# A power operation behind the gathers of a sparse message kernel, from the eleventh row block to the end

## The chip, the cores and the metric

The kernel runs on one core of a Trainium2 chip. The metric is the device time of one launch in microseconds, as the median of several runs; for the kernel before it is 361.72 us (three runs, 361.44 to 362.11). A separate execution is recorded by the hardware profiler, and all lines of profiles in this document are from such executions. The recorded execution of the kernel before took 472.48 us, with a span of 470.8 us from its first to its last instruction, so it is a good deal longer than the runs that are timed.

## The reference, cut to what matters

There are 2708 nodes with 128 features, and a matrix `adj` of 2708 x 2708 that is almost all zeros; each row holds its mean weights. Two layers follow one another.

```python
# layer 0, hyperbolic: gamma, XW per node from x and W, then
nominator   = A_hat @ (gamma * XW)
denominator = _clamp_abs(A_hat @ (gamma - 1.0))
...                                   # norms, tanh, artanh, relu
x = _layernorm(x + layer0(x, adj, W))

# layer 1, messages
s = node_feats @ msg_w[:, :D].T
d = node_feats @ msg_w[:, D:].T
messages   = gelu(s[:, None, :] + d[None, :, :] + msg_b)
aggregated = einsum('ijd,ij->id', messages, adj)
new_feats  = concatenate([node_feats, aggregated]) @ upd_w.T + upd_b
h = gelu(new_feats) + node_feats      # layernorm, weights, and once more
x = _layernorm(x + layer1(x, adj, ...))
```

The message of a pair of nodes counts only where `adj` is not zero. The kernel therefore computes messages for the edges alone.

## The kernel before, in words

The rows of `adj` are taken in 22 blocks of 128 rows.

**Layer 0 and the search for edges (loop over b = 0 to 21).** For each block, SyncE loads the transposed block `aT` (128 x 2816 in float32, 1.4 MB; L362). TensorE multiplies it with `y` into `mp` (L369, 22 products), and ScalarE takes its sign into `sgn` (L364). `keys` turns the signs into numbers whose bits name the neighbours: a product of `sgn` with powers of two, into `kx` (L396), and VectorE's MAX8 takes the largest ones into `top` (L404). `extract` works in two steps, one and two blocks later. It makes a matrix `R` that assigns each of up to 128 edges of a tile to its row, then multiplies it with the coded bits into `sel` (L489). Out of this come, for each tile t of 128 edges, the neighbour's number `J` (L500), the row's number and the weight (`rv_of`, L497), and `F`, the edge's place in the flat matrix (L501). There are 25 lists of edges (one to four per block) with 99 tiles in all.

**Two kinds of gathers**, both through the helper `gather` (L196 to L202), both indirect DMAs that GpSimd (POOL) issues:

- The **V gathers** (L505), 99 of them: 128 single numbers of `adj` at the places `F`. They serve a check only: near the end VectorE compares `V` with the weight that came out of the extraction (L848). If anything differs, a slow dense branch at the end of the program is taken. `F` has 12 buffers, so the `F` of a list can be written when the gathers of the list 12 before it have read theirs.
- The **dd gathers** (L723), 99 of them: 128 rows of 128 features of `table`, an array in HBM that holds `d`, at the numbers `J`. They feed the messages. Tiles of edges stand in 26 groups of up to four (`work`, 24 of four, one of two, one of one), and k is the place in the group. A ring of 14 groups (`RING`) holds what has been gathered and not been used. `fetch` issues up to four gathers at a time. Tiles whose neighbours all lie in the first 1280 nodes (`soon`) need only the first part of the table and may be fetched from block 14 on (`FETCH`); all others wait until the whole table has been written.

**End of layer 0.** `layer0_end` does norms and the layernorm for 10, 10 and then 2 blocks, makes `x1`, `s3` (the `s` part in three bfloat16 limbs) and the `d` part, and writes the latter to `table` (L583).

**Messages.** `messages()` takes one group: TensorE fetches `s` to the edges by `R` (L736), VectorE builds `rv`, the weight at the edge's row (L738), and adds `s` and `dd` (L741), ScalarE applies gelu (L742), and TensorE sums up with `rv` (L751). Each call then calls `fetch` and one step of the nodes' updates (`node`, `update`, `first`, `finish`), which end in the output's DMAs.

**What sets the order.** [...] The program's framework puts the instructions of an engine in a fixed order when the kernel is built, and adds the waits between engines. `gather` with `pause=True` places one more instruction directly behind its DMA: a power operation of two constant tiles of 128 x 1 on GpSimd (`gap = half ** half`), whose result nothing reads. In the kernel before, V gathers of blocks 0 to 8 are paused (61 of 99, `PAUSED = 9`), and no dd gather is.

Of the kernel before, what the change touches and what calls it, by code (L numbers as in the profile page):

```python
# [20 lines left out]
P = 128  # L21
# [7 lines left out]
CHUNKS = [(0, 10), (10, 20), (20, 22)]  # L29
PARTS = (0, 1, 2, 2)  # L30
GROUPS = [(0, 8), (8, 6), (14, 4), (18, 2), (20, 2)]
PAUSED = 9
EARLY = 8
FETCH = 14

# [3 lines left out]
SPLIT, BITS = 10, 16  # L39
# [42 lines left out]
def hyperbolic_then_message_kernel(  # L82
# [30 lines left out]
    w0_sb, wT, rowvec, o = pk[:, :D], pk[:, D : 5 * D].rearrange("p (i d) -> p i d", d=D), {}, 5 * D  # L113
# [55 lines left out]
    J = const.tile([P, NT], U32, name="J")  # L169
    V = const.tile([P, NT], F32, name="V")  # L170
# [25 lines left out]
    def gather(o, src, at, pause=False):  # L196
        last = nc.gpsimd.indirect_dma_start(  # L197
            out=o, out_offset=None, in_=src, in_offset=bass.IndirectOffsetOnAxis(ap=at, axis=0)
        )
        if pause:  # L200
            with tc.issue_after(last.ins), tc.high_priority():
                nc.gpsimd.tensor_tensor(gap, half, half, op=OP.pow)  # L202
# [10 lines left out]
    def flat(t):  # L213
        return t.rearrange("p b d -> p (b d)")
# [98 lines left out]
    for g, n in quads:  # L313
# [5 lines left out]
        t = small.tile([P, 4, D], F32, name="work", bufs=3)  # L319
        nc.vector.tensor_mul(t[:, :n, :], mx[:, g : g + n, :], mx[:, g : g + n, :])  # L320
        nc.vector.tensor_reduce(ss_m[:, g : g + n], t[:, :n, :], axis=AX.X, op=OP.add)
    for b in range(NB):
        t = small.tile([P, D], F32, name="junk")
# [89 lines left out]
    def extract(l):  # L413

        b, groups, c0, wa, wb, t0, n, late = LISTS[l]
# [34 lines left out]
        for k, _ in parts:  # L450
            first = n - late if k and wa else 0
            dl = deg[:, l, k + 1 : k + 2]
            for k0 in range(first, n, 4):
# [3 lines left out]
                o = flat(R[:, t0 + k0 : t0 + k1, :])  # L457
# [22 lines left out]
        F = small.tile([P, TMAX], U32, name="F", bufs=12)  # L480
        step = 512 // (C + 2)
        for k0 in range(0, n, step):
            k1 = min(n, k0 + step)
            w = k1 - k0
            t = slice(t0 + k0, t0 + k1)
# [16 lines left out]
                F[:, k0:k1], J[:, t], float(b * P * N - 1), rid[:, t], op0=OP.add, op1=OP.add  # L502
            )
        for t in range(t0, t0 + n):
            gather(V[:, t : t + 1], adj.rearrange("i (j o) -> (i j) o", o=1), F[:, t - t0 : t - t0 + 1], b < PAUSED)  # L505
        known[0] = b

    x1, x1T, gd = x_sb, xT, nom
# [183 lines left out]
    early, late, soon = {}, {}, set()  # L692
# [13 lines left out]
    rooms, sums, whole = [], {}, []  # L706
# [6 lines left out]
    def fetch():  # L713

        for _ in range(4):
            ready = [v for v in (True, False) if order[v] and order[v][0][0] < done[0] + RING]
            if not whole:
                ready = [v for v in ready if v and order[v][0][2] <= known[0]]
            if not ready:
                return  # L720
            q, k, _, t = order[min(ready, key=lambda v: order[v][0])].pop(0)
            while len(rooms) <= q:
                rooms.append(edge.tile([P, 4, P], F32, name="dd", bufs=RING))  # L723
            gather(rooms[q][:, k, :], table[: SPLIT * P] if t in soon else table, J[:, t : t + 1])

    def messages():

# [15 lines left out]
        for k, (b, t, first, final, before) in enumerate(ts):  # L743
# [12 lines left out]
            elif final:  # L756
                g0, gn = group[b]
                queue.append(node(gd[:, g0 : g0 + gn, :D], b - g0, b, g0, gn, [gd[:, b, :D]] if b < EARLY else []))
        fetch()
        step()  # L760
        step(1)
# [10 lines left out]
    with tc.issue_after(setup.ins):  # L772
        for b in range(NB):
            block = layer0(b)
            next(block)
            go_on(b, 0)
            for x in placed:
                next(x, None)
            placed = []
            next(block)  # L780
            go_on(b, 1)
            for x in found:
                next(x)
            placed, found = found, []
            sgn = next(block)
            for l in of_block[b]:
                keys(l, sgn)
                found.append(extract(l))
            if b == 0 or b == NB - 1:
                for x in found:  # L790
                    next(x)
                    next(x, None)
                for x in placed:
                    next(x, None)
                found, placed = [], []
            if b >= FETCH:
                fetch()
            for b0, b1 in CHUNKS:
                if b == b1 - 1 and b1 < NB:
                    ends.append((b1, layer0_end(b0, b1)))  # L800
                    next(ends[-1][1])
# [7 lines left out]
    for _ in range(RING):  # L809
        fetch()  # L810
# [25 lines left out]
    for i, v in enumerate(seconds):  # L836
        k = v.shape[1]
# [146 lines left out]
```

## Time and profile before

| | value |
|---|---|
| time, median of 3 runs | 361.72 us |
| span of the recorded execution | 470.8 us |
| mean granted TensorE clock in it | 0.787 |
| GpSimd: V gathers (99) | 98.8 us busy |
| GpSimd: dd gathers (99) | 94.8 us busy |
| GpSimd: power operations (61) | 37.8 us busy |
| DMA queue of the gathers: packets, MB, share of 16 engines | 6336, 6.55, 5.6% |
| DMA queue of SyncE | 9502, 37.43, 21.8% |

In the profile, PE is TensorE's matmuls, PEld its weight loads, DVE VectorE, ACT ScalarE, POOL GpSimd. A row of a group has the source line, engine and operation, output and input, the number of instructions; behind the bar follow busy microseconds and the mean nanoseconds of one, and behind the next bar the idle time of the engine just before them, with what ended most of it. The page's slices divide the span into 40 equal parts, and each digit is the busy share in tenths. The chain is the sequence of work that ended last, followed back from the end.

### The profile page before, as it was taken

How to read it: one execution, taken by the hardware profiler on the slowest of the kernel's cores; microseconds unless marked ns; L12 is line 12 of the kernel's file. 1: busy time of each engine (PE TensorE's matmuls, PEld its weight loads, DVE VectorE, ACT ScalarE, POOL GpSimd, SP SyncE). 2: the span in 40 equal slices, each digit the busy share in tenths (PEclk: the TensorE clock that was granted, in tenths of full speed). 3: DMA queues.
4: the chain of work that ended last, by engine and by line, in shares of the span. 5: the costliest groups of instructions: out<-in, count | busy, mean ns of one | idle time of the engine just before them, and what ended most of it. 6: DMA issues, size and time to landing. Idle time of an engine off the chain costs nothing.

```text
span 470.8 us, 8239 instructions
## 1 busy us (share of the span) xinstructions
PE 293.5 (62%) x2603; PEld 261.0 (55%) x2603; DVE 280.4 (60%) x1580; ACT 214.0 (45%) x609; POOL 242.4 (51%) x353
## 2 busy tenths in 40 slices
PE   4249999999999931252738947655300713999840
PEld 4139988999979820142627946544200712897730
DVE  0997998868979602022224779974000411799995
ACT  2953868786959802031324773932000201334441
POOL 6200888988888877735754400226776475200000
PEclk9758999999999965568957996859555665899865
DMA  8403544646644431122413300101211121100111
GB/s 335 207 1 124 194 179 135 236 142 230 222 172 158 161 117 37 28 79 95 151 28 141 126 1 24 34 11 45 52 50 50 30 54 36 24 1 4 43 37 43
DMA packets 16029, 45.15 MB, mean 96 GB/s; under 512 B 5418, under 2 KB 10942, under 8 KB 13166
## 3 DMA queue, kind: packets, MB, share of 16 engines
q1 hardware_dynamic: 9502, 37.43, 21.8%
q0 software_dynamic: 6336, 6.55, 5.6%
q10 hardware_dynamic: 144, 0.60, 0.4%
q8 instruction: 22, 0.36, 0.3%
q14 instruction: 25, 0.20, 0.1%
HBM read 41.74 MB, written 2.83 MB: 95 GB/s over the span
## 4 chain that ended last, share of the span: by engine, by line
PE 35%; DVE 27%; another core or an unknown queue 24%; ACT 6%; issue 5%; DMA 1%; DVEq 0%; ACTq 0%
PE mp L369 17%; PE kx L396 4%; PE mp L751 3%; DVE rv L738 2%; PE X L577 2%; DVE top L404 2%; PE sel L489 2%; DVE st L600 1%; PE X L736 1%; DMA xT<-in_x_t_dram 1%; DVE dd L741 1%; DVE nom L624 1%; PE kx L317 1%; PE sel L608 1%
## 5 line engine op out<-in xcount | busy, mean ns | idle before, releaser
L197 POOL DMA_INDIRECT V<-in_adj_dram,F x99 | 98.8, 998 | 108.5 <-DVE F L501 70.1
L369 PE MATMUL mp<-y,aT 128*128 128x130 f32 x968 | 141.7, 297 | 15.1 <-issue 14.8
L369 PEld LDWEIGHTS mp<-y,aT 128*128 128x128 f32 x968 | 127.1, 205 | 16.5 <-issue 16.3
L197 POOL DMA_INDIRECT dd<-table_dram,J x99 | 94.8, 958 | 47.8 <-issue 45.7
L364 ACT ACTIVATE sgn<-aT 128x2816 bf16<-128x2816 f32 x22 | 56.0, 2547 | 2.3 <-DMA aT<-in_adj_t_dram 2.1
L738 DVE TENSOR_SCALAR rv<-iotaN,rv_of 128x128 f32<-128x128 f32 x99 | 30.1, 347 | 42.8 <-PE X L736 34.2
L404 DVE MAX8 top<-kx 128x8 f32<-128x128 f32 (+3 forms) x133 | 25.3, 227 | 30.0 <-remote 25.4
L751 PE MATMUL mp<-rv,dd 128*128 128x128 f32 x198 | 35.7, 334 | 11.2 <-ACT dd L742 11.2
L489 PE MATMUL sel<-z,R 128*128 128x42 bf16 (+5 forms) x297 | 19.5, 194 | 31.6 <-issue 17.3
L202 POOL TENSOR_TENSOR gap<-gap 128x1 f32<-128x1 f32 x61 | 37.8, 620 | 1.5
L751 PEld LDWEIGHTS mp<-rv,dd 128*128 128x128 f32 x198 | 30.8, 236 | 13.4 <-ACT dd L742 12.1
L396 PE MATMUL kx<-kd,sgn 128*128 128x128 bf16 x484 | 32.9, 223 | 8.1 <-ACT sgn L364 8.1
L396 PEld LDWEIGHTS <-sgn 128*128 128x128 bf16 x484 | 28.1, 99 | 14.6 <-ACT sgn L364 8.5
L489 PEld LDWEIGHTS <-R 128*128 128x128 bf16 x297 | 15.2, 98 | 35.6 <-issue 19.6
L689 PE MATMUL mp<-ident,nom 128*128 128x128 f32 x44 | 10.0, 322 | 39.2 <-ACT nom L755 39.2
L494 DVE TENSOR_TENSOR work<-sel,place 128x120 f32<-128x120 f32 (+11 forms) x29 | 11.1, 382 | 37.4 <-remote 32.4
L742 ACT ACTIVATE dd<-dd 128x512 f32<-128x512 f32 (+2 forms) x26 | 15.8, 607 | 30.6 <-DVE dd L741 17.9
L456 ACT ACTIVATE away<-iota,mid 128x256 f16<-128x256 f32 (+3 forms) x54 | 28.7, 572 | 1.7 <-DVE mid L449 0.6
L689 PEld LDWEIGHTS mp<-ident,nom 128*128 128x128 f32 x44 | 7.1, 208 | 40.1 <-ACT nom L755 39.6
L736 PEld LDWEIGHTS <-R 128*128 128x128 bf16 x297 | 21.4, 108 | 12.4 <-issue 10.6
L755 ACT COPY nom<-mp 128x128 f32<-128x128 f32 x8 | 2.1, 262 | 46.8 <-remote 43.4
L408 ACT ACTIVATE junk_s<-kx 128x384 bf16<-128x384 f32 (+2 forms) x25 | 12.2, 486 | 18.2 <-DVE top L404 14.1
(224 smaller groups left out, 599.3 us busy)
## 6 DMA issues: line engine op xcount, KB each, us to landing
aT<-in_adj_t_dram SPq DMA_DIRECT2D x22, 1408.0 KB
V<-in_adj_dram,F POOLq DMA_INDIRECT x99
dd<-table_dram,J POOLq DMA_INDIRECT x99
xT<-in_x_t_dram SPq DMA_DIRECT2D x2, 704.0 KB
x_sb<-in_x_nm_dram SPq DMA_DIRECT2D x2, 704.0 KB
table_dram<-dt SPq DMA_DIRECT2D x4, 256.0 KB
out_dram<-nom SPq DMA_DIRECT2D x4, 256.0 KB
pk<-in_pack_dram ACTq DMA_DIRECT2D x1, 587.5 KB
```

The source lines that it names most:

```text
L197: last = nc.gpsimd.indirect_dma_start(out=o, out_offset=None, in_=src, in_offset=bass.IndirectOffsetOnAxis(ap=at, axis=0))
L202: nc.gpsimd.tensor_tensor(gap, half, half, op=OP.pow)
L364: nc.scalar.activation(sgn, aT, AF.Sign, accum_out=signs[:, b : b + 1])
L369: p = nc.tensor.matmul(op[:, : D + 2], lhsT=aT[:, j, :], rhs=y[:, j, :], start=(j == 0), stop=(j == NB - 1))
L396: nc.tensor.matmul(kp[:, i * P : (i + 1) * P], lhsT=sgn[:, j, :], rhs=kd[:, q, :], start=False, stop=(i == len(groups) - 1 and j == j1 - 1),)
L404: nc.vector.max(top[:, c : c + 8], seg[:, s, :])
L456: nc.scalar.activation(r0, iota[:, k0 * P : k1 * P], AF.Abs, scale=2.0, bias=mid[:, k : k + 1])
L489: nc.tensor.matmul(sp[:, k, :], lhsT=R[:, t0 + k0 + k, :], rhs=z[:, i, :], start=(i == 0), stop=(i == 2))
L689: nc.tensor.matmul(ag[:, :P], lhsT=gd[:, b, :D], rhs=ident, start=True, stop=False)
L736: nc.tensor.matmul(X[:, k, :], lhsT=R[:, t, :], rhs=s3[:, b, i, :], start=(i == 0), stop=(i == 2))
L738: nc.vector.tensor_scalar(rv[:, k, :], iotaN, rid[:, t : t + 1], same[:, t : t + 1], op0=OP.is_equal, op1=OP.mult)
L751: nc.tensor.matmul(sums[b][:, :P], lhsT=dd[:, k, :], rhs=rv[:, k, :], start=(first and not mine), stop=final)
```

## The change

The constant for the V gathers goes away, and both kinds of gathers get a condition of their own. V gathers of blocks 0 to 10 are all paused now, and from block 11 on those whose tile number isn't a multiple of three. Of the dd gathers, all are paused but those in place 1 of their group. The purpose is to let gathers follow one another less closely in the second half of the kernel too. What is computed stays the same.

```diff
-PAUSED = 9
...
-            gather(V[:, t : t + 1], adj.rearrange("i (j o) -> (i j) o", o=1), F[:, t - t0 : t - t0 + 1], b < PAUSED)
+            gather(V[:, t : t + 1], adj.rearrange("i (j o) -> (i j) o", o=1), F[:, t - t0 : t - t0 + 1], b < 11 or t % 3 > 0)
...
-            gather(rooms[q][:, k, :], table[: SPLIT * P] if t in soon else table, J[:, t : t + 1])
+            gather(rooms[q][:, k, :], table[: SPLIT * P] if t in soon else table, J[:, t : t + 1], k != 1)
```

## The prediction

> **What bounds the kernel now.** I read the header of the page, then engine shares and slices, the chain, the costliest groups, GpSimd's timeline, and last a table of windows. The first thing to see is that the time and the profile disagree: the median is 361.72 us, the profiled execution lasts 470.8 us, 109 us more. So the profile can't be read as it stands, and the working starts with where the 109 us sit.
>
> ```profile
> PE 293.5 (62%) x2603; PEld 261.0 (55%) x2603; DVE 280.4 (60%) x1580; ACT 214.0 (45%) x609; POOL 242.4 (51%) x353
> PE   4249999999999931252738947655300713999840
> POOL 6200888988888877735754400226776475200000
> PE 35%; DVE 27%; another core or an unknown queue 24%; ACT 6%; issue 5%; DMA 1%; DVEq 0%; ACTq 0%
> L197 POOL DMA_INDIRECT V<-in_adj_dram,F x99 | 98.8, 998 | 108.5 <-DVE F L501 70.1
> L197 POOL DMA_INDIRECT dd<-table_dram,J x99 | 94.8, 958 | 47.8 <-issue 45.7
> L202 POOL TENSOR_TENSOR gap<-gap 128x1 f32<-128x1 f32 x61 | 37.8, 620 | 1.5
> ```
>
> In the slices PE stands at 9 up to slice 14 (165 us), then falls to 1 and 2, and is back at 9 only in slices 34 to 37, when POOL shows 0. The chain names "another core or an unknown queue" for 24.1% of 470.8, or 113.5 us, though there is one core; it first appears as a long step at 164.8 us. The windows show the same:
>
> ```profile
> 84.00:120.00 36.00, 36.00 (x415) 33.85 (x416) 28.53 (x187) 27.85 (x71) 32.15 (x41) 1.00 0.55 193
> 165.00:206.00 41.00, 8.35 (x39) 6.07 (x38) 3.79 (x27) 4.04 (x16) 26.22 (x28) 0.54 0.16 52
> 320.00:370.00 50.00, 10.81 (x82) 9.98 (x80) 7.39 (x22) 2.79 (x8) 33.43 (x35) 0.58 0.17 46
> 403.00:425.00 22.00, 22.00 (x208) 19.42 (x207) 19.89 (x87) 8.45 (x26) 0.95 (x1) 0.99 0.03 7
> ```
>
> (Columns: span, then busy us of PE, PEld, DVE, ACT, POOL, then PE clock, DMA share, GB/s.) While gathers with a power operation between them run (84 to 120), PE is busy all the time. While gathers follow one another directly (165 to 206, 320 to 370), every other engine nearly stops; when they end, PE is full again. DMA is at 0.16 there, so it isn't bandwidth. But 470.8 - 113.5 = 357 us, close to the 361.7 measured without a profile. I take nearly all of this stall for something that occurs only while the profile is recorded; at most some 28 us of it (361.7 less 334, the chain without "another" and without its 5% of "issue") can be in the measured time.
>
> With the stall out, what is the bound? GpSimd is strictly serial:
>
> ```profile
> 100.41 1.00 POOL L197 DMA_INDIRECT V<-in_adj_dram,F  x1 [0.19 <-issue]
> 101.44 0.64 POOL L202 TENSOR_TENSOR gap<-gap 128x1 f32<-128x1 f32 x1
> 102.25 1.00 POOL L197 DMA_INDIRECT V<-in_adj_dram,F  x1 [0.18 <-issue]
> ...
> 340.30 0.95 POOL L197 DMA_INDIRECT dd<-table_dram,J  x1 [0.31 <-issue]
> 341.56 0.95 POOL L197 DMA_INDIRECT dd<-table_dram,J  x1 [0.30 <-issue]
> 342.81 0.95 POOL L197 DMA_INDIRECT dd<-table_dram,J  x1 [0.30 <-issue]
> ```
>
> From start to start a bare gather takes 1.26 us (the median of all direct successors), one with a power operation 1.80 us (the median of the 61). GpSimd's first V gather is at 47.6 us. Until the table in HBM is complete it has 99 V gathers (61 of them paused) and 40 early dd gathers to issue (so many stand before 300 us in its timeline): 61 x 1.80 + 78 x 1.26 = 208 us, so it is done at 256. When is the table complete? The first gather after it is at 318.9 in the trace. Row block 15 of layer 0 ends at 162; undisturbed blocks take 8 us, so block 21 would end near 210 to 220 rather than at 277.3, which puts the table at 252 to 262: GpSimd is just done by then. After it come 59 dd gathers: 59 x 1.26 = 74 us. The last quad's tail (its add at 448.3 to the end at 470.8) is 22.5, and I put 2 us, an estimate, for landing. 261 + 74 + 24.5 gives 360: the measured time comes out if **GpSimd's gathers are the bound of the message stage**. The other engines need less: PE, the busiest, shows 82 us from 300 to 449, part of them at a clock of 0.6, against 74 from the gathers alone plus their late start.
>
> **What the Trainium skill says.** "Perfetto Trace Analysis", section "GPSIMD Engine Instruction", says to time GpSimd by start-to-start spacing, since the reported spans don't compose; the trace agrees (spans of 0.95 leave 0.30 us each that belong to the gather), so I use 1.26 and 1.80. Its section "DMA Instruction — SWDGE (GPSIMD)" says a gather's reported end is the end of descriptor generation, not of the data movement; the trace fits, as the next gather starts 0.30 us after it. "DMA: Bandwidth & Descriptors", section "SWDGE vs HWDGE vs iDMA", says gathers and plain loads use different queues in each DMA engine, served in turn, so the aT stream can go on beside the gathers: 193 GB/s from 84 to 120 agrees. No page prices this power operation; the trace does.
>
> **The change part by part.** Counts from the lists in the code. (1) V gathers of blocks 9 and 10: 7, all newly paused. (2) Blocks 11 to 21: 31 V gathers, of which 21 have t % 3 > 0. So 28 more V pauses. (3) dd gathers: in 26 groups (24 of four, one of two, one of one) all but k = 1: 99 - 25 = 74 pauses, 31 of them behind the 40 early gathers and 43 behind the 59 after the table. Sum: 102 added, none removed. Each costs 1.80 - 1.26 = 0.54 us of GpSimd time, from the two spacings.
>
> Nobody reads the result of the power operation; what waits is what is queued behind it on GpSimd: the next gather. Before the table: (28 + 31) x 0.54 = 31.9 us, ending at 256 + 32 = 288. V itself is needed only by the comparison at L848, which sits in DVE's queue among the first messages, so a late V holds DVE there too; but the late dd gathers, queued behind the V gathers, are what sets the end. Part of the 31.9 lies in GpSimd's slack before the table. The measured time gives the slack: 361.7 - 24.5 - 74.3 = 263 for the table, 7 us after 256. So 25 us reach the path. After the table: 43 x 0.54 = 23.2 us, all on the path, since GpSimd gives a quad every 4 x 1.26 = 5.0 us before and 3 x 1.80 + 1.26 = 6.7 us after, while the engines handled the last 13 groups, once their data was there, in 46 us (403 to 449), 3.5 us each. The ring of 14 groups doesn't hide it: it lets GpSimd run ahead, but GpSimd is behind. Total 361.7 + 25 + 23 = **409 us**. Deleting the constant costs nothing. No wait is added on other engines by name; F tiles (12 buffers) are freed later, but DVE needs the buffer of list 12 only after list 0's gathers, and GpSimd is then fewer than 12 lists behind.
>
> What isn't known is the spacing with no profile recorded. Upper bound: as in the trace with no slack, 102 x 0.54 = 55, giving 417. Lower: the gaps of 0.30 and 0.17 belong to the recording, leaving 0.96 per gather and 0.60 per power operation. Then all of GpSimd's work is 198 x 0.96 + 163 x 0.60 = 288 us; 47.6 + 288 + 24.5 = 360 if it never waits, and with 82 us after a table at 257 it is 364. I take the trace's spacing, since the same page shows memsets 0.03 us apart, so recording doesn't put a gap before every GpSimd instruction.
>
> **The rivals.**
> - *Only the part after the table counts.* GpSimd has enough slack before it (its spacing is smaller, or the table later). 361.7 + 23 = 385. For it: the waits of V on F, 70 us, show that GpSimd can catch up; against: they fall in stretches in which DVE is stalled.
> - *The gaps vanish without a profile*: 360 to 372, no change at the lower end. For it: two spacings of 0.30 and 0.17 with no cause in the trace; against: the memsets, and that 1.26 reproduces 361.7.
> - *Faster.* The stall that direct gathers bring is in the measured time, up to 28 us, and the pauses take it away. For it: the table of windows, where the only difference between full and starved engines is the power operation. Against: the pauses still fill GpSimd, and the floor just worked out is 360, so a real gain needs shorter GpSimd operations than the trace has; with 5% off 288 it is 346, and I put 353, the mean of both, an estimate.
>
> **How the numbers follow.** Likeliest, GpSimd in full: 0.53 (409). Only the part after the table, or partly: 0.16 (380 to 398). No gaps, slower: 0.12 (362.5 to 380). Within 0.2% (361.0 to 362.4): 0.03. Faster: 0.16 (353). That makes slower 0.81. The range goes from 361, which leaves out the faster case, to the upper bound 417, with some 0.03 beyond it.
>
> **What would show it.** In the profile after: x163 in the L202 row at about 0.6 us; the dd row's direct spacing replaced by 1.80 on three of four; POOL busy near 242 + 102 x 0.6 = 304 us; the chain of the last third led by POOL or by waits of DVE dd on gathers, and "another core or an unknown queue" far below 24%, so the profiled span may well shrink while the measured time grows. I am wrong if the measured time is under 370: then either the spacing of 1.26 belongs to the recording, or the stall is real. I am wrong on the first part alone if it is near 385.

## The result and the profile after

The kernel after takes **417.15 us** (median of 4, 416.39 to 417.48) against 361.92 us before in the same comparison: a ratio of 1.1517, 95% interval 1.1483 to 1.1551, or 55.2 us more. The forecast was 409 us, in a range of 361 to 417, so the measured time lies at the range's upper edge.

One thing must be known to read all that follows. The kernel before has two times, which go with the chip that runs it: 361.9, 363.9 and 363.2 us in three comparisons, 481.2, 477.0 and 479.8 us in three others. The experiments met four chips, two of each kind, and none of them showed both times. The profile that the prediction read (470.8 us) fits the second kind, the timed 361.72 the first. The kernel after takes 416 to 417 us on both.

The page of the kernel after, the lines that answer to those shown of before (lines of the code are one lower now):

```profile
PE 282.2 (68%) x2603; PEld 255.3 (61%) x2603; DVE 282.0 (68%) x1580; ACT 213.7 (51%) x609; POOL 308.8 (74%) x455
PE   3419999999998999999837462001754887865630
POOL 6400389888888888887888888888888888888500
PE 33%; POOL 24%; DVE 16%; DMA 13%; ACT 7%; issue 5%; POOLq 0%; DVEq 0%; SPq 0%; ACTq 0%
L196 POOL DMA_INDIRECT V<-in_adj_dram,F x99 | 99.3, 1003 | 51.6 <-DVE F L500 32.4
L196 POOL DMA_INDIRECT dd<-table_dram,J x99 | 99.5, 1005 | 21.4 <-issue 20.0
L201 POOL TENSOR_TENSOR gap<-gap 128x1 f32<-128x1 f32 x163 | 99.0, 608 | 5.5
```

POOL is the one engine whose slices have no hole from slice 6 to slice 37, and it has become the second entry of the chain, where before it did not appear at all. The power operations are 163 at 608 ns. The entry "another core or an unknown queue", 24% of the chain before, is gone. This page shows none of the hold-up that the profile of before shows, so part of that difference is the chip's and not the change's: recorded later on a chip where before takes 477 us, the kernel after has 17% POOL in its chain and 7% of the unnamed entry. The idle time of PE in slices 25 to 28 has another cause now. The longest waits of the kernel after:

```profile
ACT dd L741 <- DVE dd L740: 84.3, 17, 38.8
PE X L735 <- DVE dd L740: 41.3, 3, 37.6
DVE work L847 <- DMA V<-in_adj_dram,F: 38.3, 1, 38.3
DVE dd L740 <- DMA dd<-table_dram,J: 34.2, 11, 5.8
```

(Who waited for whom, microseconds in all, times, the longest.) VectorE stands for 38.3 us at the comparison of V, because the last V gather comes late, and does nothing else in that time; ScalarE and TensorE wait behind VectorE. After that, VectorE waits for the gathers of the messages, 34.2 us in 11 pieces. Both go back to GpSimd, whose timeline at that point reads:

```profile
284.61 0.95 POOL L196 DMA_INDIRECT V<-in_adj_dram,F  x1 [0.30 <-issue]
285.59 6.37 POOL L201 TENSOR_TENSOR gap<-gap 128x1 f32<-128x1 f32 x10
292.21 1.00 POOL L196 DMA_INDIRECT dd<-table_dram,J  x1 [0.26 <-issue]
293.24 0.59 POOL L201 TENSOR_TENSOR gap<-gap 128x1 f32<-128x1 f32 x1
294.01 0.99 POOL L196 DMA_INDIRECT dd<-table_dram,J  x1 [0.17 <-issue]
```

The last part of the table was sent at 246.2 us, but the first gather that needs it starts at 292.2. The ten power operations in a row are more than one gather's: not every pause stands directly behind its own gather. In the order that the framework gave the kernel after, 15 of the 163 have moved to this row and to two rows of four shortly before it, where one takes some 0.64 us. The early dd gathers that they belong to, among the V gathers from 174 us on, follow one another directly, up to seven in a row. That does little to the time here, but it will matter on the other kind of chip. From 292.2 to the start of the last gather at 389.8 pass 97.6 us for 60 gathers, then 26.0 us to the end at 415.8.

### The profile page after: what moved, and what is told of

The parts are those of the page before. It is cut to its first block, busy times and chain, and to the rows that moved or that the text cites. A ratio compares the mean times of both kernels' runs of the same rounds, so it can differ in the third digit from the quotient of the medians.

```text
span 415.8 us, 8341 instructions
## 1 busy us (share of the span) xinstructions
PE 282.2 (68%) x2603; PEld 255.3 (61%) x2603; DVE 282.0 (68%) x1580; ACT 213.7 (51%) x609; POOL 308.8 (74%) x455
## 4 chain that ended last, share of the span: by engine, by line
PE 33%; POOL 24%; DVE 16%; DMA 13%; ACT 7%; issue 5%; POOLq 0%; DVEq 0%; SPq 0%; ACTq 0%
PE mp L368 18%; POOL dd L196 10%; POOL gap L201 9%; DMA aT<-in_adj_t_dram 7%; POOL V L196 5%; DMA dd<-table_dram,J 5%; PE kx L395 4%; ACT sgn L363 3%; PE sel L488 2%; PE mp L750 2%; PE X L576 2%; DMA xT<-in_x_t_dram 1%; PE kx L316 1%; DVE dd L740 1%; DVE st L555 1%
## 5 line engine op out<-in xcount | busy, mean ns | idle before, releaser
L368 PE MATMUL mp<-y,aT 128*128 128x130 f32 x968 | 128.6, 284 | 0.0
L368 PEld LDWEIGHTS mp<-y,aT 128*128 128x128 f32 x968 | 117.5, 194 | 0.3
L196 POOL DMA_INDIRECT dd<-table_dram,J x99 | 99.5, 1005 | 21.4 <-issue 20.0
L201 POOL TENSOR_TENSOR gap<-gap 128x1 f32<-128x1 f32 x163 | 99.0, 608 | 5.5
L750 PE MATMUL mp<-rv,dd 128*128 128x128 f32 x198 | 37.6, 346 | 25.4 <-ACT dd L741 25.3
L750 PEld LDWEIGHTS mp<-rv,dd 128*128 128x128 f32 x198 | 32.1, 244 | 28.3 <-ACT dd L741 27.6
L735 PE MATMUL X<-s,R 128*128 128x128 bf16 x198 | 18.1, 240 | 41.3 <-DVE dd L740 41.3
L455 ACT ACTIVATE away<-iota,mid 128x256 f16<-128x256 f32 (+3 forms) x54 | 28.5, 571 | 2.0 <-DVE mid L448 1.5
L740 DVE TENSOR_TENSOR dd<-X,dd 128x512 f32<-128x512 f32 (+1 forms) x17 | 11.4, 670 | 24.6 <-DMA dd<-table_dram,J 20.5
L847 DVE TENSOR_TENSOR work<-V,rv_of 128x99 f32<-128x99 f32 x1 | 0.3, 261 | 38.3 <-DMA V<-in_adj_dram,F 38.3
L740 DVE TENSOR_TENSOR dd<-kx,dd 128x512 f32<-128x512 f32 (+1 forms) x9 | 5.8, 647 | 15.3 <-DMA dd<-table_dram,J 13.8
```

Of the source, the lines that this page charges most:

```text
L196: last = nc.gpsimd.indirect_dma_start(out=o, out_offset=None, in_=src, in_offset=bass.IndirectOffsetOnAxis(ap=at, axis=0))
L368: p = nc.tensor.matmul(op[:, : D + 2], lhsT=aT[:, j, :], rhs=y[:, j, :], start=(j == 0), stop=(j == NB - 1))
L455: nc.scalar.activation(r0, iota[:, k0 * P : k1 * P], AF.Abs, scale=2.0, bias=mid[:, k : k + 1])
L735: nc.tensor.matmul(X[:, k, :], lhsT=R[:, t, :], rhs=s3[:, b, i, :], start=(i == 0), stop=(i == 2))
L740: nc.vector.tensor_tensor(dd, X, dd, op=OP.add)
L750: nc.tensor.matmul(sums[b][:, :P], lhsT=dd[:, k, :], rhs=rv[:, k, :], start=(first and not mine), stop=final)
```

## The experiments

Theory A: GpSimd is one serial chain from its first gather at 47 us to its last, and each pause adds the difference of the two spacings (from the start of one gather to the start of the next, with and without a pause between). The rivals differ in what is hidden and in what the stall of the recorded kernel before is.

### One half of the change at a time

The first has the new condition for V gathers alone, the second for dd gathers alone.

```diff
 # v_part
-            gather(rooms[q][:, k, :], ..., J[:, t : t + 1], k != 1)
+            gather(rooms[q][:, k, :], ..., J[:, t : t + 1])
 # dd_part
-            gather(V[:, t : t + 1], ..., b < 11 or t % 3 > 0)
+            gather(V[:, t : t + 1], ..., b < 9)
```

> Only the V gathers get the new condition (89 paused), dd gathers none. Theory A, GpSimd is a serial chain from its first gather to its last and has no slack: 28 more pauses of 0.54 us each, 361.9 + 15 = 377. Rival B, GpSimd has the 7 us of slack before the table that the prediction took: 370. Rival C, only the part after the table counts: 362.

> Only the dd gathers get the new condition (74 paused), V gathers as before (61). Theory A: 74 x 0.54 = 40 us, 402. Rival B: 7 us of it hidden, 395. Rival C, only the part after the table: some 24 us, 386. If A holds, the two parts add up to the whole change (55 us).

Measured: 379.44 us for the V half, ratio 1.042 (1.037 to 1.047) to 363.9 of before on the same chip, so 15.5 us for 28 pauses (A: 15). The dd half took 401.78 us, ratio 1.106 (1.102 to 1.111), so 37.9 us for 74 pauses (A: 40). Together 53.4 of the 55.2 us. That is 0.55 and 0.51 us for a pause, and no slack of 7 us is to be seen in either half. The rivals B and C fall.

### No pauses, and short ones

```diff
 # no_pause: both conditions False
 # short_pause, from the kernel after
-                nc.gpsimd.tensor_tensor(gap, half, half, op=OP.pow)
+                nc.gpsimd.memset(gap, 1.0)
```

> No power operation at all. Theory A (the stall beside direct gathers belongs to the recording): GpSimd is done with 99 V and 39 early dd gathers at 47.6 + 138 x 1.26 = 222, waits for the table until some 249, then 60 x 1.26 = 76 and a tail of 26: 351 timed, while the recorded span grows to well over 470. Rival D (the stall is real to a part): the time is not under 362, and above it if the stall grows with the number of direct gathers.

> As the kernel after, but each of the 163 power operations is a memset of the same 128 x 1 tile, which took 0.09 us where the profile of before shows it. Theory A (the duration counts): 0.04 us each instead of 0.54, 44 of them after the table, so 351 + 2 = 353. Rival E (any instruction between two gathers brings the wait, whatever it lasts): near 417. The recorded span shows besides whether a short instruction keeps the other engines from stalling (span near the timed 353) or only the length of the power operation does (span well over 400).

Measured on the same chip: 354.72 us without pauses, ratio 0.977 (0.973 to 0.981), and 358.47 us with short ones, ratio 0.981 (0.974 to 0.988, from three of its four runs). Both timed figures are near those of theory A (351 and 353), 4 and 5 us above them. But the second half of A, that the recorded span would grow, was wrong: the span is 351.6 us without pauses and 356.5 with short ones. Here is the window from 165 to 206 us of the kernel without pauses (span, then busy us of PE, PEld, DVE, ACT, POOL, PE clock, DMA share, GB/s):

```profile
165.00:206.00 41.00, 39.33 (x432) 36.90 (x431) 31.79 (x208) 31.61 (x83) 31.25 (x33) 1.00 0.58 195
```

PE is busy 39.33 of 41 us beside direct gathers, recorded and all; in the profile of before it was 8.35 in the same stretch. So recording alone is not what stalls the engines. And for the time that a pause adds, the length of the instruction counts, not its presence: with the short one, the spacing of gathers is 1.25 us as without any.

### The kernel before, recorded again

> The kernel before, unchanged, recorded a second time. Theory A1 (the stall beside direct gathers is not a property of the kernel, since the run without any pause did not show it): the span is near the timed 362 and no step of the chain is named another core or an unknown queue. Rival D2 (this arrangement of paused and direct gathers stalls whenever it is recorded): the span is near 470 again. GpSimd then starts its first gather after the table at 254 or later (61 x 1.80 + 77 x 1.26 after 47.6), though the table is complete by about 249.

This kernel, the next two and the one with two power operations ran on another chip, and there the kernel before took 478.35 us timed, its companion runs 481.2, with a span of 474.7 us. The span near 470 is D2's, but neither A1 nor D2 foresaw that the stall is in the timed runs too. (The first gather after the table starts at 320.3 us here, because the table itself is late, sent by 318.0; so whether GpSimd alone would have been ready by 254 is not tested by this run.) The chain and the window show the picture of the prediction's profile again:

```profile
PE 35%; DVE 22%; another core or an unknown queue 20%; issue 9%; ACT 8%; DMA 5%; DVEq 0%; ACTq 0%; SPq 0%
165.00:206.00 41.00, 9.51 (x46) 8.27 (x46) 4.75 (x32) 5.06 (x18) 25.95 (x28) 0.51 0.18 56
```

### Without V gathers, with and without pauses

```diff
 # no_v, from the kernel after
-            gather(V[:, t : t + 1], ...)
+            pass
+    nc.vector.tensor_copy(V, same)          # ahead of the comparison
 # no_v_no_pause: besides
-            gather(rooms[q][:, k, :], ..., J[:, t : t + 1], k != 1)
+            gather(rooms[q][:, k, :], ..., J[:, t : t + 1])
```

> The kernel after without its 99 V gathers and the pauses behind them; V is filled with a copy of the weights, so the check of the weights is left out. Theory A: GpSimd reaches the table in time, the gathers after it start at 249 rather than 292: 60 of them, 44 paused, take 44 x 1.79 + 16 x 1.26 = 99, and the tail 26: 374, 43 less than the kernel after. Rival F (the pauses of the V gathers lie beside other work, and only the messages' own pauses count): about 417, as after, or a few us less.

> As the one before it (no V gathers, the check of the weights left out), and no pause behind the dd gathers either. Theory A: the table sets the start (249) and 60 x 1.25 = 75 and the tail of 26 follow: 350, no less than some 3 us under the kernel without pauses (354.7), whose 99 V gathers were hidden before the table. Rival F: the V gathers take time of the path wherever they stand, 20 us or more are saved (under 335).

Both ran on the chip on which the kernel before takes 481 us. Without V gathers but with the dd pauses: 375.81 us (A: 374). Its GpSimd timeline shows when the table is complete:

```profile
219.03 0.89 POOL L201 TENSOR_TENSOR gap<-gap 128x1 f32<-128x1 f32 x1
249.94 1.06 POOL L196 DMA_INDIRECT dd<-table_dram,J  x1 [30.03 <-DMA table_dram<-dt]
```

GpSimd is idle for 30 us and goes on at 249.9, when the table's DMA has landed. In the kernel after this gather starts at 292.2, so 42.3 us of backlog come between, and the times differ by 415.79 - 375.81 = 40.0 us (the kernel after as measured below on a chip of the same kind). Rival F falls for this case.

Without the dd pauses as well: 452.74 us, where A said 350 and F under 335. The one run against the other, on the same chip: taking 74 pauses **away** costs 77 us. The chain names "another core or an unknown queue" for 22% there, and not at all with the pauses. The same stretch, with the pauses and then without:

```profile
165.00:206.00 41.00, 36.91 (x397) 34.17 (x396) 30.62 (x195) 28.98 (x72) 35.31 (x44) 1.00 0.53 184
165.00:206.00 41.00, 5.81 (x21) 2.69 (x22) 0.11 (x1) 0.02 (x1) 29.30 (x31) 0.50 0.20 51
```

Both have dd gathers alone in it, so the V gathers are not needed for the stall. As a test of A against F on the V gathers it is inconclusive, since the stall covers everything; for the stall it is the clearest pair of all.

### Two power operations

```diff
                 nc.gpsimd.tensor_tensor(gap, half, half, op=OP.pow)
+                nc.gpsimd.tensor_tensor(gap, half, half, op=OP.pow)
```

> The kernel after with the power operation issued twice behind each of the 163 paused gathers. Theory A: each adds its spacing of 0.61 to 0.62 us (runs of four took 2.48 us in the profile after), all on GpSimd's chain: 417 + 163 x 0.62 = 518. Rival G (GpSimd has waits of its own, on landings or on the ring, that a longer pause would fill): well under 518, for instance 470.

Measured: 503.20 us, on the chip with the stall; 15 us under A and far from G. The trace explains the 15: the last gather starts at 471.1, and a row of power operations follows it, the last at

```profile
490.57 0.55 POOL L202 TENSOR_TENSOR gap<-gap 128x1 f32<-128x1 f32 x1
```

with nothing behind it. The framework's order left these 18 us of pauses for the end, so they delay no gather. What does stand ahead of the last gather is paid in full: it is 135 operations more than in the kernel after, and the last gather starts 84 us later than in that kernel on a chip of the same kind (386.9, shown below), 0.62 us each.

### The kernel after and the short pauses, again

> The kernel after, unchanged, a second time, since the kernel before took 364 us beside the first four experiments and 481 us beside the next four, which ran on another chip. Theory H (on some chips direct gathers hold up the other engines, recorded or not, and pauses of this length prevent it): the kernel after is near 417 wherever it runs; where the kernel before is near 480 it is faster than that by some 13%, where before is near 364 it is slower by 15%. Rival I (the second chip slows everything by a third): where before is near 480, after is near 550.

> The kernel with a memset of 0.12 us in place of each power operation, unchanged, a second time. Its spacing of 1.25 to 1.30 us is that of direct gathers. Theory H with the spacing as the cause: where before is near 480, this one stalls through all of its gathers and takes over 480. Rival J (any instruction of another kind between two gathers prevents the stall): 358 wherever it runs, and this would be better than both. Where before is near 364, both theories give 358.

These met a chip on which before takes 363.15 us: 416.25 us for the kernel after, ratio 1.145 (1.142 to 1.148), and 355.68 us for short pauses, ratio 0.981 (0.976 to 0.986). Nothing is told apart, as the expectation said for this case; both repeat the earlier values within 1%.

> The kernel after, unchanged, a third time; the second time it met a chip on which the kernel before takes 363 us. Theory H: near 417 wherever it runs; where before is near 480 that makes it some 13% faster. Rival I: near 550 where before is near 480. Where before is near 363 nothing is told apart.

> The kernel with a memset of 0.12 us in place of each power operation, unchanged, a third time; so far it ran only where the kernel before takes 363 to 364 us. Where before is near 480: theory H with the spacing as the cause says it stalls through all its gathers, over 480; rival J (any instruction of another kind in between prevents the stall) says 358. Where before is near 363 nothing is told apart.

These two ran one by one, and each met a chip with the stall. The kernel after: 415.79 us against 477.03 of before, ratio **0.873** (0.860 to 0.887). Short pauses: 526.20 us against 479.76, ratio 1.097 (1.063 to 1.131). So theory H holds, and I and J fall: the same kernel with a memset of 0.12 us between its gathers takes 356 us on one chip and 526 on the other, while the kernel after doesn't mind. The window of 84 to 120 us lies in the same stage in the three recordings shown here, since their gathers begin at 46.6 to 48.2 us. First the short pauses on the chip with the stall, then the kernel before on that same chip, which has power operations there, then the short pauses on a chip without the stall:

```profile
84.00:120.00 36.00, 26.09 (x230) 24.12 (x229) 17.54 (x106) 17.95 (x47) 21.71 (x40) 0.78 0.24 82
84.00:120.00 36.00, 35.94 (x408) 33.52 (x407) 28.21 (x185) 27.74 (x72) 32.08 (x41) 1.00 0.53 182
84.00:120.00 36.00, 35.68 (x407) 33.20 (x406) 28.54 (x181) 26.89 (x71) 30.68 (x58) 1.00 0.53 186
```

VectorE is busy 17.5 us in the first and 28.2 and 28.5 in the others. Its two longest waits in the first recording are for "remote", that is, for a releaser that the profile can't name:

```profile
DVE rv L737 <- remote: 41.0, 3, 30.8
DVE top L403 <- remote: 37.1, 9, 14.8
```

The kernel after isn't wholly free of it either. Recorded on a chip with the stall, its window from 165 to 206 us is

```profile
165.00:206.00 41.00, 24.55 (x194) 20.84 (x190) 13.33 (x78) 13.92 (x40) 33.74 (x40) 0.71 0.31 98
```

with PE at 24.6 us, against 39.7 on the chip without. The moved pauses fit this. Up to 172 us nearly every gather is followed by a power operation. After that come four rows of four to seven gathers without one, 1.25 us apart, which end at 181.1, 193.4, 224.4 and 238.4 us. The unnamed entry has four steps in the chain of this recording (start, length), each in such a row or at its end:

```profile
180.07 9.13 another core or an unknown queue
193.30 10.18 another core or an unknown queue
219.18 3.26 another core or an unknown queue
237.10 5.43 another core or an unknown queue
```

Ten microseconds ahead of the first row, and ten from the second row on:

```profile
155.00:165.00 10.00, 9.88 (x111) 9.33 (x111) 7.79 (x51) 9.43 (x30) 8.92 (x12) 1.00 0.64 239
185.00:195.00 10.00, 4.36 (x23) 3.60 (x23) 2.95 (x21) 2.18 (x8) 7.94 (x10) 0.50 0.16 41
```

PE falls from 9.9 of 10 us to 4.4, though the kernel has its pauses elsewhere. That the moved pauses are the reason is not shown: it is a coincidence in time within one recording, and no run has them put back. In all, the stall costs this kernel nothing because GpSimd, which sets the end, is busy throughout: its last V gather starts at 281.7 and its last dd gather at 386.9 us, as on the other chip (284.6 and 389.8).

No version that was run is the best on both. Where direct gathers do no harm, the kernel without pauses is faster than both kernels of the change, by 2.3% (1.9 to 2.7) and, against the kernel after in other comparisons, some 15%. Where they do harm, the kernel after is the fastest of those that were run there and compute everything.

## Why the prediction was right, and where it was wrong

**The spacings.** 1.26 us direct and 1.80 us paused were read from the trace of before. The kernel after shows medians of 1.30 (50 direct successors) and 1.79 us (144 with one power operation between). That they hold without a profile is shown by the halves of the change, 0.55 and 0.51 us for a pause against 0.54. The rival in which the gaps of 0.30 us vanish is refuted by this, too.

**After the table.** 59 gathers with 43 pauses were counted, and it is 60 with 44. The stretch was to grow from 74.3 by 23.2 to 97.5 us; it is 97.6.

**Before the table, the step that was mis-sized.** The prediction charged 25 of 31.9 us, since it gave GpSimd 7 us of slack. It got them by taking the tail and the gathers off the measured time, which put the table at 263 us. The table is complete at 249.9. GpSimd was due at 256, so it was late already in the kernel before, and each pause ahead of the table counts. With all 102 pauses at 0.54 us the sum is 55 us and the time 417, the upper bound of the prediction, which is what was measured. Two other runs without the stall agree. The V half starts its first gather after the table at 274.2 us; without its 28 added pauses of 0.54 us that is 259 for the kernel before, an estimate. The kernel without pauses starts it at 249.7 and is 9.2 us faster than before. So GpSimd was some 9 us late, where the prediction had it 7 us early. The sum 256 + 76 + 26 = 358 falls some 4 us short of the kernel before; 3 of them are the 259, the other is not traced, since that kernel was never recorded on a chip without the stall.

**The stall, the step that was wrong.** "I take nearly all of this stall for something that occurs only while the profile is recorded" is refuted by two runs: 351.6 us recorded without any pause, and 478 us timed with the kernel before. The subtraction of 113.5 us was right for the chip on which the time was taken, but for a reason that wasn't the true one: that it led to 357 us, near the measured time, was luck. Its rival, "the stall that direct gathers bring is in the measured time", was given 353 us and is false on the chips of 362 us; on the others it is right and larger than foreseen, 61 us of gain where at most 28 us of stall were allowed for. Which of the two kinds of chip times the change was not to be seen in one profile; that the profiled span and the time differed by 109 us was the sign that two conditions had been mixed.

**The signs that were named.** The count of 163 and 608 ns, the busy POOL (308.8 for 304) and the chain with POOL in it came as said; so did the lower span. The "only the part after the table" rival (385) falls with the V half.

## What to carry to other kernels

A pause on an engine that only issues transfers is free only as long as that engine keeps its lead: add up its instructions start to start, up to the first point where others wait for it, and compare with when the data it needs is ready. If a profile and the timed runs of a kernel differ by a quarter, find out first, by running the same kernel again elsewhere, whether they are of the same condition; an explanation that needs the recording to be the cause should be tested with one more recording. Where an added instruction is to stand behind a certain other one, look in the timeline whether it does: 15 of 163 did not here. And judge a remedy on the chips that have the ailment: the same pauses are worth minus 15% here and plus 13% there.

## What the runs showed of the hardware

- On two of the four chips that the experiments met, gathers issued by GpSimd every 1.25 us hold up the other engines' progress (short pauses, 526 us); on the other two they don't (356 to 358 us). The spacing of the gathers is the same on both, and their DMA traffic is small (6.6% to 8.3% of the engines' span in the runs without the stall, 5.5% to 7.3% on the chips with it). With power operations between them, 1.79 us apart, the hold-up is mostly gone (375.81 us with them and 452.74 without, on one chip and without V gathers). What it is made of stays open: the waits are for releasers that the profile doesn't name, and no run tells whether it is semaphores or something else. Two more things are not shown. The pauses that prevent the stall are all power operations and the one that doesn't is a memset of 0.12 us, so the spacing and the kind of instruction were never varied apart; a memset as long as a power operation would tell. And that the chip is the cause, rather than something that went with it, rests on four chips, of which one was met twice with the same result (481.2 and 479.8 us).
- A memset of 128 x 1 between two gathers costs nothing on GpSimd in these runs: it takes 0.12 us and the spacing stays at 1.25. A power operation on the same 128 elements takes 0.59 to 0.61 us and adds 0.54.
